# One core, two layers of graph attention: the last element's stores in four pieces, and new step lists for the first three and last two elements

## The chip, the cores and the metric

The kernel runs on one core of a Trainium2 chip. The metric is the device time of one execution in microseconds (us), lower is better. All data are fp32. The engines are called PE (TensorE, the matmuls), DVE (VectorE), ACT (ScalarE), POOL (GpSimd) and SP (SyncE, which here issues every transfer).

## The reference

`x` is 32 elements of 512 rows by 512 columns, `adj` 32 matrices of 512 by 512. Layer 0 is attention in 8 heads of 64 columns with a bias from the adjacency, an output projection, a residual and a layer norm. Layer 1 is graph attention on the same adjacency.

```python
# layer 0
q, k, v = x @ Wq.T + bq, x @ Wk.T + bk, x @ Wv.T + bv        # split into 8 heads of 64
logits = q @ k^T / 8 + log(clip(adj, 1e-8))                  # per head
out = (softmax(logits) @ v) @ Wo.T + bo
x = layer_norm(x + out) * gamma + beta
# layer 1
f = x @ fc_w.T + fc_b
logits = (f @ q_w + q_b) + (f @ k_w + k_b)^T
masked = logits + (1 - adj) * -1e9
atten = softmax(where(masked >= 0, masked, 0.01 * masked))
out = atten @ f + x
```

## The kernel before

The elements are worked through one after the other, with layer 1 one element and its output two elements behind layer 0. Products of 512 by 512 are done in seven half-size products instead of eight (Strassen's scheme), which is why there are many sums of quarters on DVE. The log of the adjacency is not formed: `exp(logits)` is multiplied by the clipped adjacency instead (`factor`, L947, on DVE).

Nothing is scheduled by a program: `fast` (L582) runs under a manual schedule, and each engine executes its instructions in the order in which they are written out. For each element two lists are run, by `first_two(b, order)` (L1427, heads 0 to 3) and `second_two(b, order)` (L1461, heads 4 to 7, and what belongs to the element before and the one after). A list is a string of step names; `perform` (L1405) calls one step after the other. A step issues between one and some 40 instructions on its engines. PE, DVE, ACT and SP each work strictly in order, so a step that waits holds everything that stands behind it on its engine. SP issues all transfers, so a load that must wait for its buffer holds the loads behind it.

Elements 2 to 30 use the lists `FIRST` and `SECOND`. Element 0 uses `FIRST0` and `SECOND0`, element 1 `FIRST1` and `SECOND1`, and element 31 `FIRST_LAST` and `SECOND_LAST`. The last one also does layer 1 of element 30 and, at its end, the whole of layer 1 of element 31.

The names that the change and the prediction use:

- `S0` to `S7`: the scores of a pair of heads for a quarter of the rows (PE, L935) and their exponential on ACT (L942, L944). `f` followed by head pair and quarter: `factor` (DVE, L950). `s` and `t`: the sums by which the softmax is divided (DVE, L962 to L973). `V0a`, `V0b`, `V0e` and so on: attention times values (PE, L1007) and its copy (ACT, L1016).
- `x`, `d`, `q`, `Q`, `p`, `v`: transposes, differences, and the products q and k of the pairs (`qm1` and on) and v (`vm1` to `vm7`) of the next element. `w` and `W`: the output projection. `n`, `k`, `u`: normalise rows (ACT, L414) and dot products for layer 1; `kst` and `kld`: the row of k goes to memory and comes back on all partitions (L448).
- `la`: the adjacency into `cT` in 16 transfers of 64 KB in pieces of 128 bytes; `c0` to `c3`: its turn (DVE, L683). `le0`, `le1`: the rows of the adjacency for layer 1 into `L` (L134), `mk0`, `mk1`: its masks (DVE, L455), `lg`, `lk`, `nm`, `ex`, `inv`, `nr`: layer 1's softmax. `ldn`: the rows of x for the residual. `lwv`, `lwk`, `lwq`, `lwo`, `lfc`: the weights; `lf`, `lv`, `lq0`, `lk0`, `lbo`, `lcc`, `lgamma`: vectors; `g`, `h`, `r`, `R`, `D`, `G`, `O`, `B`, `P`: sums of weights and folds of vectors into them.
- In the last list `om` and `oa`: the output product of element 29, `H`: the division of the last head pairs, `J`, `Z`, `Y`, `O`: layer 1 of element 30, names with a leading `x`: the layer-1 softmax of element 31, names with a leading `L` its products (`last_steps`, L1203), of which `Lo...` are the output steps of `last_out_steps` (L1319) and `Lot0` and on the stores. `rg0` to `rg2` compute a flag: if a sum fell outside a safe range, the elements are done again by `general`, which does not happen with these inputs.

Of the kernel before, what the change touches and what calls it, by code (L numbers as in the profile page):

```python
# [19 lines left out]
P = 128  # L20
# [10 lines left out]
def kernel(  # L31
# [550 lines left out]
    def fast(ctx):  # L582
# [736 lines left out]
        def last_out_steps(b, banks, x, fcs):  # L1319
# [25 lines left out]
            def store(row, count, j):  # L1345
                nc.sync.dma_start(
                    out=out[b][row * P : (row + count) * P, ts(j, H)].rearrange(
                        "(c p) d -> p c d", p=P),
                    in_=yb[:, row : row + count, ts(j, H)],
                )  # L1350
            return {
# [5 lines left out]
                "b11": lambda: add_rows(1, 1, "a"), "t0": lambda: store(2, 2, 1),  # L1357
                "b10": lambda: add_rows(1, 0, "a"), "t1": lambda: store(2, 2, 0),
                "m20": lambda: mul(2, "b", ns=(0,)),
                "b01": lambda: add_rows(0, 1, "c"), "t2": lambda: store(0, 2, 1),  # L1360
                "a000": lambda: add_rows(0, 0, "b", range(1)), "t3": lambda: store(0, 1, 0),
                "m21": lambda: mul(2, "d", ns=(1,)),
                "a001": lambda: add_rows(0, 0, "d", range(1, 2)), "t4": lambda: store(1, 1, 0),
# [145 lines left out]
        def end_steps(b, banks):  # L1509
# [48 lines left out]
            "ob11 ot0 ob10 ot1 om20 ob01 ot2 oa000 ot3 om21 oa001 ot4"  # L1558
# [37 lines left out]
            f30 f20 d3 lv1 r3 d2 f32 f23 f21 qcb qm6 f33 qm2 f31 qcq2 O0 mv0 qcq1
            vm5 V2a la V2b G1 qck2 vcb vc22 qm3 s20 qaq2 O1 qm7 dv0 vm6 V2e G2 vc12
            s21 vm3 va12 qak2 V3a Qm1 O2 Qcb c1 V3b s30 vm2 qm4 Qm6 qck1 Qm5 vm7 Qm2
            Qck2 c2 Qm4 s31 Qcq1 c3 Qm3 s32 s22 V3e va22 t20 Qcq2 vm4 G0 R0 sc01 Qm7
            Qck1 Qaq2 vc11 c0 sc00 Qak1 vc21 Qak2  # L1600
        """
        FIRST1 = """
            t21 S0 t30 t31 S1 S2 S3 S4 S5 mv2 S6 f00 S7 f01 f02 V0a qm1 f03 V0b G3
            R1 f13 f12 qcb qm6 V0e dv2 qm2 f10 qcq2 qcq1 f11 qm5 B1 qck2 P1 ldn P0
            P2 wseed s00 s01 qm3 qaq2 qm7 qak2 s02 V1a wm1 V1b t00 Qm1 fd wcb qm4
            Qcb sc20 sc21 qck1 fs wm2 ws11 R2 s10 Qm5 R3 s11 wm5 wa11 ws12 wm6 wm3
            wa01 wm7 t01 Qck2 wb01 wa00 ldx Qm6 Qm2 b0 wb11 s12 wm4 V1e b1 wa10 Qm4
# [25 lines left out]
            os12 V3e le0 H33 om7 oa11 H34 om3 Wal ob11 kld om4 ldn Wseed sc00 sc01
# [180 lines left out]
```

## Time and profile before

| what | us |
| --- | --- |
| median of three runs | 3275.07 (3274.25 to 3275.76) |
| profiled execution | 3278.6 |
| its span, first to last instruction | 3277.0 |
| PE busy | 3255.5 |
| DVE busy | 3077.4 |
| ACT busy | 1479.1 |
| mean granted PE clock | 0.999 of full speed |

The span is what the profile covers; the profiled execution's own time lies 1.6 us above it. A line of the timeline gives start and length in us, the engine, the line of the code, the operation, the tiles (output, then inputs) with their shape, how many instructions the group holds, and in brackets how long the engine was idle before it and who ended that. Matmuls overlap, so a group's starts tell more than its lengths: two groups of 16 matmuls of 256 columns follow each other at 1.73 us.

### The profile page before, as it was taken

How to read it: one execution, taken by the hardware profiler on the slowest of the kernel's cores; microseconds unless marked ns; L12 is line 12 of the kernel's file. 1: busy time of each engine (PE TensorE's matmuls, PEld its weight loads, DVE VectorE, ACT ScalarE, POOL GpSimd, SP SyncE). 2: the span in 40 equal slices, each digit the busy share in tenths (PEclk: the TensorE clock that was granted, in tenths of full speed). 3: DMA queues.
4: the chain of work that ended last, by engine and by line, in shares of the span. 5: the costliest groups of instructions: out<-in, count | busy, mean ns of one | idle time of the engine just before them, and what ended most of it. 6: DMA issues, size and time to landing. Idle time of an engine off the chain costs nothing.

```text
span 3277.0 us, 64102 instructions
## 1 busy us (share of the span) xinstructions
PE 3255.5 (99%) x25590; PEld 1886.2 (58%) x25590; DVE 3077.4 (94%) x5323; ACT 1479.1 (45%) x2770; POOL 1.4 (0%) x15
## 2 busy tenths in 40 slices
PE   9999999999999999999999999999999999999998
PEld 4555555555555555555556555555555555555555
DVE  7999999999999999999999999999999999999997
ACT  3445444445444354344444444544435444444443
POOL 0000000000000000000000000000000000000000
PEclk9999999999999999999999999999999999999999
DMA  5343433443433434334443345343343433443412
GB/s 133 51 70 86 74 83 66 77 96 64 89 68 69 96 70 89 73 68 86 89 71 84 67 76 96 64 91 73 62 96 72 88 76 64 86 92 69 86 46 78
DMA packets 917264, 256.46 MB, mean 78 GB/s; under 512 B 842720, under 2 KB 844768, under 8 KB 916960
## 3 DMA queue, kind: packets, MB, share of 16 engines
q1 hardware_dynamic: 916960, 252.30, 38.9%
q8 instruction: 204, 3.34, 0.4%
q14 instruction: 100, 0.82, 0.1%
HBM read 184.00 MB, written 36.72 MB: 67 GB/s over the span
## 4 chain that ended last, share of the span: by engine, by line
PE 97%; SPq 1%; DVE 1%; DMA 1%; ACT 0%; issue 0%; DVEq 0%
PE f L221 23%; PE mz L221 15%; PE my L221 15%; PE mx L221 15%; PE po L1007 14%; PE sc L935 7%; PE mx L935 2%; PE my L935 2%; PE mz L935 2%; SPq L620 0%; DMA L<-in_q_w_dram 0%; PE mx L350 0%; PE ps L1072 0%; SPq L134 0%; DMA L<-in_adj_dram 0%
## 5 line engine op out<-in xcount | busy, mean ns | idle before, releaser
L950 DVE SCALAR_TENSOR_TENSOR at<-cT,at 128x1024 f32<-128x1024 f32 x512 | 611.0, 1217 | 0.7 <-ACT at L944 0.5
L1007 PE MATMUL po<-at,v 128*64 128x512 f32 x2048 | 485.6, 595 | 0.7 <-ACT oT L1016 0.7
L739 ACT ACTIVATE qT<-f,bq 128x256 f32<-128x256 f32 x254 | 116.2, 472 | 816.7 <-PE f L221 816.6
L962 DVE TENSOR_TENSOR at<-at,at 128x1024 f32<-128x1024 f32 x378 | 455.2, 1211 | 3.7 <-PE po L1007 3.5
L1007 PEld LDWEIGHTS po<-at,v 128*64 128x64 f32 x2048 | 141.3, 137 | 225.0 <-issue 131.5
L221 PE MATMUL f<-xT,wq 128*64 128x256 f32 x2032 | 262.6, 379 | 0.5 <-ACT at L944 0.5
L944 ACT ACTIVATE at<-sc 128x1024 f32<-128x1024 f32 x256 | 259.7, 1079 | 4.6 <-PE sc L935 4.2
L221 PE MATMUL f<-T,qk_s 128*64 128x256 f32 x2032 | 256.3, 379 | 0.8 <-ACT kT L739 0.7
L935 PE MATMUL sc<-qT,kT 64*128 64x512 f32 x1024 | 242.3, 589 | 0.0
L221 PEld LDWEIGHTS f<-xT,wq 128*64 128x64 f32 x2032 | 145.7, 137 | 102.7 <-issue 36.7
L221 PEld LDWEIGHTS f<-T,qk_s 128*64 128x64 f32 x2032 | 145.5, 137 | 87.9 <-issue 17.1
L739 ACT ACTIVATE kT<-f,bk 128x256 f32<-128x256 f32 x254 | 120.5, 474 | 119.5 <-PE f L221 118.1
L935 PEld LDWEIGHTS sc<-qT,kT 64*128 64x128 f32 x1024 | 99.8, 187 | 120.3 <-issue 76.5
L966 DVE STREAM_TRANSPOSE at<-at 128x1024 f32<-128x1024 f32 x126 | 154.8, 1229 | 1.1
L973 DVE TENSOR_REDUCE ks<-at 128x32 f32<-128x1024 f32 x126 | 152.2, 1208 | 1.0
L935 PE MATMUL so<-qT,kT 64*128 64x512 f32 x256 | 137.1, 615 | 0.0
L935 PE MATMUL mx<-qT,kT 64*128 64x512 f32 x256 | 132.7, 598 | 1.2 <-ACT v L802 0.7
L935 PE MATMUL mz<-qT,kT 64*128 64x512 f32 x256 | 132.6, 598 | 0.0
L935 PE MATMUL my<-qT,kT 64*128 64x512 f32 x256 | 132.4, 597 | 0.2 <-ACT v L802 0.2
L221 PE MATMUL f<-T,wk 128*64 128x256 f32 x1016 | 131.3, 379 | 0.0
L221 PE MATMUL f<-xT,wk 128*64 128x256 f32 x1016 | 131.3, 379 | 0.0
L221 PE MATMUL f<-xT,qk_s 128*64 128x256 f32 x1016 | 131.3, 379 | 0.0
(391 smaller groups left out, 6397.7 us busy)
## 6 DMA issues: line engine op xcount, KB each, us to landing
cT<-in_adj_dram SPq DMA_DIRECT2D x512, 64.0 KB
R<-d SPq DMA_DIRECT2D x126, 256.0 KB
x<-in_x_dram SPq DMA_DIRECT2D x124, 256.0 KB
L<-in_adj_dram SPq DMA_DIRECT2D x62, 512.0 KB
n<-in_x_dram SPq DMA_DIRECT2D x31, 1024.0 KB
out_dram<-yb SPq DMA_DIRECT2D x62, 512.0 KB
eP<-L SPq DMA_DIRECT2D x480, 64.0 KB
w<-dk SPq DMA_DIRECT2D x32, 256.0 KB
```

The source lines that it names most:

```text
L221: nc.tensor.matmul(to[ts(h, DK)], left[:, ts(h, DK)], right, start=start, stop=stop, skip_group_check=True,)
L739: nc.scalar.activation(of(w, half), ps[bank], AF.Identity, bias=bias)
L935: nc.tensor.matmul(parts[j], s["kT", p][rows, ts(kc, P)], s["qT", p][rows, :], start=True, stop=True,)
L944: nc.scalar.activation(at, sc, AF.Exp, scale=SCALE)
L950: nc.vector.scalar_tensor_tensor(at, cT[:, kc, :].unsqueeze(1).to_broadcast([P, 2, N]), ADJ_MIN, at, ALU.max, ALU.mult,)
L962: nc.vector.tensor_add(to, to, s["at", p, kc])
L966: nc.vector.transpose(flat, flat)
L973: nc.vector.tensor_reduce(ks.rearrange("p h m -> p (h m)"), flat.rearrange("p (a k) -> p a k", k=BL), AX.X, ALU.add,)
L1007: nc.tensor.matmul(s["po", p][j * DK : (j + 1) * DK, :], s["v"][h // 4][:, kc, ts(h % 4, DK)], s["at", p, kc][:, j, :], start=(kc == 0), s ...
```

## The change

The stores of the last element go out in four pieces instead of five, three of them changed in shape: rows 2 and 3 whole, row 1 right, row 0 whole, row 1 left (a "row" is 128 rows of the matrix). The six special lists are laid anew. The steps are the same but for the store that is gone; some steps stand in another list (the loads `lv1`, `lf0`, `lv2`, `lgamma` and the folds `r2`, `D6`, `D7`, `O2`, `R0`, `G0`, `G2`).

```diff
-            def store(row, count, j):
+            def store(row, count, cols):
                 nc.sync.dma_start(
-                    out=out[b][row * P : (row + count) * P, ts(j, H)].rearrange(
+                    out=out[b][row * P : (row + count) * P, cols].rearrange(
                         "(c p) d -> p c d", p=P),
-                    in_=yb[:, row : row + count, ts(j, H)],
+                    in_=yb[:, row : row + count, cols],
                 )
+            whole, left, right = slice(0, D), slice(0, H), slice(H, D)
...
-                "b11": lambda: add_rows(1, 1, "a"), "t0": lambda: store(2, 2, 1),
-                "b10": lambda: add_rows(1, 0, "a"), "t1": lambda: store(2, 2, 0),
+                "b11": lambda: add_rows(1, 1, "a"), "b10": lambda: add_rows(1, 0, "a"),
+                "t0": lambda: store(2, 2, whole),
                 "m20": lambda: mul(2, "b", ns=(0,)),
-                "b01": lambda: add_rows(0, 1, "c"), "t2": lambda: store(0, 2, 1),
-                "a000": lambda: add_rows(0, 0, "b", range(1)), "t3": lambda: store(0, 1, 0),
+                "b01": lambda: add_rows(0, 1, "c"), "t2": lambda: store(1, 1, right),
+                "a000": lambda: add_rows(0, 0, "b", range(1)), "t3": lambda: store(0, 1, whole),
                 "m21": lambda: mul(2, "d", ns=(1,)),
-                "a001": lambda: add_rows(0, 0, "d", range(1, 2)), "t4": lambda: store(1, 1, 0),
+                "a001": lambda: add_rows(0, 0, "d", range(1, 2)), "t4": lambda: store(1, 1, left),
...
         FIRST0 = """
-            X0 X1 X2 X3 E1 E0 E2 E3 A0 lwv A1 d0 g0 lwk vm1 vm5 vcb d1 g3 d3 lgamma
-            la3 lwq lf2 g1 vm6 vc22 vm2 d2 vc12 lq0 g2 g4 la2 vm7 vm3 la0 va22 c3
-            vm4 vc21 lbo vc11 lwo S0 c2 va12 S1 S2 S3 h0 pm1 h4 pm5 h1 c0 h3 pcb f00
-            lfc pck2 r0 pm6 h2 lf1 D0 pm2 pm4 lv0 pm3 la1 pcq2 pcq1 D1 pm7 pck1 D2
-            paq2 pak1 S4 r1 c1 S5 pak2 S6 S7 D3 f01 Bq f03 f02 V0a V0b V0e f10 qm1
-            qcb qm5 D4 qck2 f13 f12 f11 qm6 qm2 s00 qm3 D5 s01 qcq1 B0 s02 D6 lv2
-            qcq2 qm7 qak2 r2 D7 lk0 V1a V1b V1e qaq2 t00 s10 lcc qm4 qck1 Qm1 Qcb
-            s11 s12 Qm5 Qm6 Qm2 Qck2 Qm4 Qcq1 t01 Qcq2 Qm3 Qm7 Qck1 ldx Qak1 Qak2
-            Qaq2
+            X0 X1 X2 X3 E0 E1 E3 E2 A0 lwv g0 A1 g1 d0 la1 d1 vm1 g3 lwk d2 vcb g2
+            vm5 g4 lwo h0 vm6 d3 vm2 vc12 lwq vm7 vc11 vc22 vm3 va22 la0 vm4 vc21 S0
+            c0 va12 S1 S2 h4 S3 pm1 h1 pm5 la2 h2 pcb pck2 lfc pm6 lf1 h3 lf0 pm2 D0
+            pcq1 pm4 pcq2 D1 la3 c3 lf2 pm3 f03 pck1 c1 paq2 lv0 pm7 pak1 S4 pak2 S5
+            S6 S7 Bq qm1 f01 c2 r0 qm5 lbo D2 f10 qcb qm6 f11 qm2 f12 f00 V0a f02
+            f13 V0b D3 s00 qcq1 lv1 qcq2 qm7 B0 lcc s01 qck2 V0e qak2 s02 qm3 qaq2
+            t00 V1a V1b lq0 Qm1 s10 D4 qm4 Qcb ldx s11 Qm6 D5 qck1 V1e Qm5 Qck2 Qm2
+            Qcq2 Qm4 s12 Qm3 Qcq1 t01 lk0 Qck1 Qm7 r1 Qak2 Qaq2 Qak1
         """
         SECOND0 = """
-            S0 x0 t10 x3 lf0 S1 x1 t11 S2 d0 f22 S3 S4 S5 S6 S7 Oq x2 d1 qm1 vm1 qm5
-            f30 f20 d3 lv1 r3 d2 f32 f23 f21 qcb qm6 f33 qm2 f31 qcq2 O0 mv0 qcq1
-            vm5 V2a la V2b G1 qck2 vcb vc22 qm3 s20 qaq2 O1 qm7 dv0 vm6 V2e G2 vc12
-            s21 vm3 va12 qak2 V3a Qm1 O2 Qcb c1 V3b s30 vm2 qm4 Qm6 qck1 Qm5 vm7 Qm2
-            Qck2 c2 Qm4 s31 Qcq1 c3 Qm3 s32 s22 V3e va22 t20 Qcq2 vm4 G0 R0 sc01 Qm7
-            Qck1 Qaq2 vc11 c0 sc00 Qak1 vc21 Qak2
+            x0 S0 S1 t10 t11 f20 S2 x1 S3 S4 f21 d0 S5 lv2 S6 S7 f22 x3 Oq f31 D6 x2
+            d1 qm1 qm5 f30 mv0 dv0 f23 qck2 qcb r3 O0 V2a vm1 qm3 qm6 V2b d3 f33 qm2
+            G1 vcb vm6 qcq1 qcq2 qaq2 V2e D7 qm7 V3a Qm1 s20 Qcb f32 qak2 sc01 d2
+            V3b vc12 qm4 qck1 vm7 s30 Qm6 vm5 vc22 la Qm5 Qck2 c0 Qm2 Qcq2 Qm4 Qcq1
+            sc00 c1 s21 Qm3 s22 c2 Qm7 V3e O1 Qck1 c3 va22 s31 t20 Qak1 vm4 vm3 vc21
+            vm2 s32 va12 vc11 Qaq2 Qak2
         """
         FIRST1 = """
-            t21 S0 t30 t31 S1 S2 S3 S4 S5 mv2 S6 f00 S7 f01 f02 V0a qm1 f03 V0b G3
-            R1 f13 f12 qcb qm6 V0e dv2 qm2 f10 qcq2 qcq1 f11 qm5 B1 qck2 P1 ldn P0
-            P2 wseed s00 s01 qm3 qaq2 qm7 qak2 s02 V1a wm1 V1b t00 Qm1 fd wcb qm4
-            Qcb sc20 sc21 qck1 fs wm2 ws11 R2 s10 Qm5 R3 s11 wm5 wa11 ws12 wm6 wm3
-            wa01 wm7 t01 Qck2 wb01 wa00 ldx Qm6 Qm2 b0 wb11 s12 wm4 V1e b1 wa10 Qm4
-            Qcq1 b2 Qm3 b3 Qcq2 Qck1 Qaq2 Qm7 Qak2 Qak1
+            fd t30 S0 S1 t21 t31 mv2 f01 S2 S3 S4 f00 S5 f02 G0 S6 O2 S7 f03 B1 ldn
+            P0 f10 wseed V0a V0b qm1 dv2 s00 f12 s01 qcb V0e f13 qm5 qck2 qm6 qm2
+            qm3 P1 qcq2 f11 P2 qcq1 s02 wm1 qm7 V1a wcb qak2 r2 G2 V1b qaq2 G3 qm4
+            sc21 sc20 fs ws11 R0 R3 Qm1 R1 t00 wm5 wm2 ldx wa11 wm6 ws12 qck1 Qcb
+            t01 wa00 wm3 R2 Qm6 wa01 s10 wb01 wm7 Qm5 s11 Qck2 wb11 b0 Qm2 Qcq1 b1
+            s12 wm4 Qcq2 wa10 b2 b3 Qm4 Qm3 Qck1 Qaq2 Qm7 Qak1 Qak2 V1e
         """
         SECOND1 = """
-            x0 n0 t10 S0 x2 t11 mv0 S1 S2 x1 S3 n2 f23 d0 S4 f20 n1 x3 S5 le1 k0 S6
-            n3 f32 vm1 k1 k2 n4 k3 vm5 u0 S7 qm1 k4 le0 qcb d1 vcb qm5 d3 qck2 kst
-            u1 f33 kld qm6 u3 u2 qm3 vm6 f21 f22 qm2 u4 V2a vm2 dv0 mk1 qcq2 f31 V2b
-            vc22 V2e f30 vc12 s20 mk0 qcq1 d2 lg0 lg1 lg2 lg3 lk0 V3a vm3 nm ex0 lk3
-            qm7 ex3 vc11 V3b vm7 va12 lk1 ex1 qaq2 la qak2 lk2 Qm1 qm4 Qcb ex2 s30
-            sc00 qck1 inv Qm5 nr0 nr3 va22 nr1 s31 sc01 Qm6 Qm2 nr2 Qck2 Qm4 vm4 s21
-            Qcq2 c0 s22 c2 Qcq1 c1 Qm3 Qck1 bl t20 Qaq2 s32 Qm7 Qak2 Qak1 vc21 c3
-            V3e
+            t10 n0 x0 x1 S0 S1 t11 S2 n2 S3 S4 S5 S6 f22 n3 d0 n1 n4 f21 le1 vm1 S7
+            qm1 x3 qcb vcb k1 qm5 x2 k0 d1 qm6 k2 d2 k3 qck2 u0 qm2 k4 vm6 u2 d3 mv0
+            le0 kst f32 qcq2 kld mk0 qcq1 qm3 u1 qm7 vm5 vc22 vc12 f30 qak2 qaq2 u3
+            dv0 Qm1 f20 f33 Qcb u4 f23 lg0 lg1 f31 mk1 qm4 V2a V2b V2e vm2 qck1 Qm6
+            Qm2 V3a Qm5 lk1 lg2 lg3 lk2 lk3 nm s20 ex3 ex1 ex2 la c0 lk0 ex0 sc00
+            Qcq2 Qck2 s21 V3b inv vm7 nr1 Qm4 Qcq1 Qm3 s22 va22 s30 V3e c1 s31 vm3
+            Qm7 nr0 nr2 vm4 va12 Qck1 Qaq2 s32 nr3 vc21 bl t20 Qak1 c2 lgamma Qak2
+            sc01 c3 vc11
         """
         FIRST_LAST = """
-            t21 S0 t30 f00 S1 S2 f01 t31 S3 S4 S5 S6 S7 V0a qm1 f02 y0 e2 qcb e0 qm5
-            e1 qck2 e3 qm6 qm2 zt1 qm3 qcq2 zm1 zs1 f10 qaq2 zcb f13 zm5 zA21 Qm1
-            zE11 mv2 zA11 zE12 zc22 zm2 zm6 dv2 qcq1 zE21 f03 qm7 zc12 V0b f11 zm7
-            fd Qcb y1 s00 zA12 f12 Qm6 za22 V0e s01 sc21 sc20 fs qak2 zc11 V1a zm3
-            za12 zm4 zc21 V1b wseed wm1 s10 s11 V1e ws11 ldn s02 wcb t00 wm5 wm2
-            wa11 qm4 ws12 wm6 wa01 wm3 wa00 qck1 wb01 t01 b0 wm7 wb11 Qm2 s12 b1 Qm5
-            Qcq1 Qck2 wm4 wa10 b2 Qm4 Qcq2 Qm3 b3 Qm7 Qck1 Qaq2 Qak2 Qak1
+            S0 S1 t21 f00 t30 f01 S2 S3 S4 S5 t31 f02 S6 S7 V0a qm1 y0 e1 qm5 qcb
+            qm6 qm2 qcq1 e0 mv2 zm1 f03 e2 V0b e3 zs1 zt1 zcb qcq2 zm5 zE11 zA21 dv2
+            zE12 qck2 qm3 qaq2 f11 zA11 zm2 f10 f13 y1 zA12 zE21 Qm1 qm7 Qcb Qm6 V0e
+            zm6 V1a sc21 zc12 zc22 s00 qak2 zm7 za22 zm3 sc20 zc11 f12 zm4 fd V1b
+            za12 ldn s01 zc21 fs Qm2 wseed s10 s11 wm1 ws11 wm5 wcb s02 wm6 wm2 t00
+            qm4 Qcq1 wa11 wa01 qck1 ws12 s12 wm7 wm3 wa00 t01 Qm5 Qck2 wb11 wm4 wb01
+            b0 Qm4 b1 wa10 Qcq2 b2 Qm3 V1e Qck1 b3 Qaq2 Qm7 Qak1 Qak2
         """
         SECOND_LAST = """
-            n0 S0 S1 S2 S3 t10 zd S4 S5 oseed f21 f20 n1 S6 n2 f23 f31 t11 f22 S7 n3
-            V2a zs f30 om1 H20 k1 V2b n4 k0 mv0 ocb k3 om2 k2 f32 k4 V2e u0 os11 u1
-            H30 H21 kst om6 V3a u3 u2 dv0 u4 f33 H31 H22 H32 H23 V3b oa01 om5 H24
-            os12 V3e le0 H33 om7 oa11 H34 om3 Wal ob11 kld om4 ldn Wseed sc00 sc01
-            Wfd mk0 Wm1 Wfs lg1 le1 lg0 Wcb lk1 Ws11 lk0 mk1 lg3 lg2 Wm5 Wm6 Wm2
-            Wa01 nm Wa11 lk2 ex1 ex0 Wm7 Ws12 Lal lk3 Wb11 ex2 ex3 inv nr2 oa10 Wm3
-            Wa00 oa00 nr0 ob01 Wb01 Wm4 Wa10 nr1 nr3 J0 J1 J2 b0 J3 b1 b2 b3 xle0
-            xmk0 xn0 xn2 xn4 xn1 xn3 xk1 xk3 xk0 Z0 Z1 Z2 xk2 xle1 ost1 ost0 yn
-            Oseed xk4 xkst xu1 y1 Z3 xmk1 xkld Om1 xu0 xu3 xu2 xu4 Yd y0 Ys xlg0
-            Os11 xlg1 Om5 Ocb xlg2 Om6 Oa11 xlg3 Oa01 xlk3 xnm Om2 xex3 xlk0 Om7
-            Os12 xlk2 xlk1 xex0 Ob11 xex2 xex1 xinv Om3 LN2 xnr0 Om4 xnr3 Lp0 Oa10
-            xnr1 LN0 Lp1 LN1 xnr2 Oa00 Lp2 Lp3 Le0 Ob01 Le1 Le2 Lm1 Le3 LT0 Lm5 Lcb
-            LT1 LT3 Lm6 Lc12 LT2 Lc22 Lm7 Ly Lm2 Lc11 LN3 La22 Lm4 Lm3 La12 LZ2 LZ0
-            Ost1 Lc21 Loseed Lom1 Lom4 Locb LZ1 Lom6 LZ3 Loa01 rg0 Lom5 Lom21 Loa001
-            rg1 Loa10 Lom7 Loa11 Lob11 Lob10 rg2 Ost0 Lom3 Lob01 Lom20 Lot4 Lot0
-            Loa000 Lot1 Lot2 Lot3
+            n0 zd S0 f20 S1 S2 t10 S3 f22 n1 f21 zs f23 S4 S5 S6 ldn t11 k0 n2 k1 n3
+            k2 oseed S7 V2a H20 mv0 f30 n4 V2b k3 om1 u0 os11 ocb u1 u2 u3 dv0 H21
+            u4 V2e f31 k4 om6 om2 oa01 om5 os12 H22 kst f32 le0 H30 oa11 om7 f33 H23
+            V3a H31 H32 ob11 sc00 Wal sc01 kld V3b om3 V3e om4 xle0 Wfd H24 xle1 le1
+            H33 Wseed mk0 Lal H34 Wfs lg0 lg1 lk0 lk1 Wm1 Wm5 Ws11 Wcb Wm6 mk1 Wm2
+            lg3 lg2 Wa01 Wm7 nm ex1 lk2 ex0 Wa11 Ws12 lk3 Wb11 Wm3 oa10 ex2 ex3 inv
+            nr0 ob01 nr2 nr1 Wm4 Wa00 Wb01 oa00 ost0 Wa10 nr3 J0 b0 b1 b2 J1 J2 b3
+            xn0 J3 xmk1 xn2 xk1 xn1 xk0 xn4 xk3 ost1 xn3 yn Z0 xk2 xk4 xkst xu1 xu0
+            xkld Z1 Z2 y0 Yd Oseed xu3 xu2 y1 Z3 Om1 xu4 xmk0 Ys xlg1 Os11 Om5 Ocb
+            xlk1 Om6 xlg0 xlg3 Oa11 Oa01 xlg2 xlk3 xnm xex3 xex1 Om2 Os12 xlk2 Om7
+            xlk0 Om3 Ob11 LN0 xex2 Om4 xex0 xinv xnr0 Oa10 xnr1 Ob01 LN2 Lp0 xnr2
+            Ost1 Lp1 xnr3 Lp2 Lp3 Le0 Oa00 Le1 Le2 Le3 LT0 Lm1 Lm5 Ost0 LT1 LN1 rg0
+            Lcb Lm6 LT2 LN3 LT3 Lc12 Lc22 Ly Lm7 Lm2 La22 Lm4 Lm3 La12 LZ0 Lc11 LZ1
+            Lc21 Loseed Lom1 Lom4 rg1 LZ2 Locb LZ3 Loa10 Lom6 Loa01 Lom5 Lom7 Loa11
+            Lob11 Lob10 rg2 Lot0 Lom3 Lob01 Lot2 Lom20 Lom21 Loa000 Lot3 Loa001 Lot4
         """
```

## The prediction

> **What bounds the kernel now.** I read the page first (busy shares, chain), then the windows of the stretches whose lists change, then the waits of the tensor engine (PE), and last the timelines around each wait and around the last loads and stores.
>
> ```profile
> PE 3255.5 (99%) x25590; PEld 1886.2 (58%) x25590; DVE 3077.4 (94%) x5323; ACT 1479.1 (45%) x2770; POOL 1.4 (0%) x15
> PE 97%; SPq 1%; DVE 1%; DMA 1%; ACT 0%; issue 0%; DVEq 0%
> 0.00:45.00 45.00, 39.21 (x236) 21.76 (x240) 23.28 (x38) 15.16 (x26) 1.36 (x15) 1.00 0.83 215
> 110.00:220.00 110.00, 106.16 (x772) 58.44 (x770) 103.49 (x179) 52.97 (x98) 0.00 (x0) 0.98 0.35 58
> 220.00:320.70 100.70, 100.61 (x800) 58.41 (x798) 95.51 (x166) 45.81 (x86) 0.00 (x0) 1.00 0.40 79
> 3200.00:3230.00 30.00, 27.42 (x148) 14.97 (x148) 26.13 (x64) 16.93 (x32) 0.00 (x0) 1.00 0.25 91
> ```
>
> The last four lines are windows: stretch, length, then busy time of PE, weight loads, DVE, ACT, POOL, the granted clock, DMA share and GB/s. A steady element (220 to 320.7) keeps PE busy 100.61 of 100.70 us. The change touches no steady list, so those 29 elements (2 to 30) give nothing and take nothing. What can move lies at the two ends: PE is idle 5.8 us in the first 45 us, 3.84 us in 110:220 (mostly element 1's second list), 2.58 us in 3200:3230, and the stretch after the last matmul. The waits say for what:
>
> ```profile
> PE my L221 <- ACT at L942: 2.2, 1, 2.2
> PE pw_a L221 <- DVE n L866: 1.5, 1, 1.5
> PE pw_a L221 <- DVE oT L862: 0.9, 1, 0.9
> PE my L221 <- DVE eT L1258: 0.8, 1, 0.8
> ```
>
> Read: what PE ran when the wait ended, who released it, total us, times, longest. All are single events, so each belongs to one place in one special list. PE does the same work per list before and after (sums of its rows are equal list by list: 56.85, 39.81, 40.26, 37.91, 50.00 and 98.92 us), so the time moves only by waits, the clock and the drain.
>
> **Part 1, element 1's second list: about -2.5 us.** The dearest wait is followed by slow matmuls:
>
> ```profile
> 152.61 1.02 PE L935 MATMUL sc<-qT,kT 64*128 64x512 f32 x4
> 155.81 3.62 PE L221 MATMUL my<-wv,xT 128*64 128x256 f32 x16 [2.17 <-ACT at L942]
> 159.26 1.89 PE L221 MATMUL mz<-v_s,T 128*64 128x256 f32 x16
> 152.25 0.85 ACT L414 ACTIVATE n<-n,rt,rstd 128x512 f32<-128x512 f32 x1
> 153.91 0.87 ACT L414 ACTIVATE n<-n,rt,rstd 128x512 f32<-128x512 f32 x1
> 155.10 0.66 ACT L942 ACTIVATE at<-my 128x512 f32<-128x512 f32 x1
> ```
>
> vm1 (the first value product, 155.81) writes the bank "my" that the exponential of S5 still reads (155.10 to 155.76); ACT reaches that one late because two normalise rows (n2 and n1, 0.85 and 0.87 us) stand ahead of it in its queue. After the wait the 16 matmuls take 3.62 us where the next such group takes 1.89: half clock, 1.73 us more, which is also the 0.98 of the window. By starts against the pitch of a group that does not wait (1.73 us for 16 of these matmuls), the losses of the list are 2.6 at 155.81, 0.45 at 163.33, 1.06 at 174.58 and 184.96 each, 0.3 and 0.8 before 192.50, and 0.5 at 200.05; with the 1.73 that is 8.5 us.
>
> In the changed list one normalise row fewer stands ahead of that exponential, so vm1 loses about 1 us less, 1.6. But the new order does not run free: walking it with the rows' durations (DVE: factor 1.22, sum 1.21, transpose 1.21, reduce 1.19; ACT: 0.47 to 1.08) I find DVE behind at V2a and V2b (waits for f20 and f23, about 0.75 and 0.6), qm5 about 0.5, and vm4 standing last, so that the next element's S0 waits for its sum, about 0.9. V0b in element 1's first list, with O2's 1.95 us moved ahead of it, waits about 0.4. That is 1.6 + 0.75 + 0.6 + 0.5 + 0.9 + 0.4 = 4.75 in place of 8.5. DVE limits the rest of it: it ends the last turn of the adjacency (c3) at 192.8 instead of 194.9 by the walk, so element 2's first value product comes at 197.5 instead of 200.05. I take that -2.5; bounds -1 (DVE further behind than walked) and -3.75 (the difference of the losses in full).
>
> The half clock is uncertain. In these rows an idle time of 2.17 us is followed by 3.4 us at half clock, and one of 1.49 us at 3206 is followed by a group of 1.95, at full clock. With about 1.5 us left I expect none. [...]
>
> **Part 2, the loads of element 0: 0.** wv, wk, wq, wo, fc and the four pieces of the adjacency go through SP in another order, with the same bytes. PE's waits there (0.69 at 30.25, 0.49 at 34.45, 0.53 at 41.30) are for ACT and DVE, none for a load, and I find the same three in the new order. Cover: before, the loads landed wv 13.1, wk 16.4, la3 18.1, wq 21.8, la2 26.3, la0 28.2, wo 34.6, fc 37.4, la1 39.7. Keeping these lengths, the new order puts wq at 23 to 25, la0 25 to 27, la2 27 to 29.5, fc 30 to 33, la3 33 to 37. la3's turn (c3) now stands ahead of the DVE sums that S4 needs (41.30); it must land by about 38.8. If it lands later, each us costs one. The steps that change lists (the loads lv1, lv2, lf0 and lgamma, small rows; the folds O2, r2, R0 on DVE and G0, G2 on ACT, now in element 1's first list; D6 and D7 in element 0's second) keep their rows and stand in stretches where DVE is ahead of PE, apart from the O2 counted above; uncovered, each fold would cost at most its own 1 to 2 us.
>
> **Part 3, the last two elements: about -3.5 us.** The tail waits for rows of the adjacency:
>
> ```profile
> 3191.40 1.90 PE L221 MATMUL mz<-fc,third 128*64 128x256 f32 x16
> 3191.61 0.41 SPq L134 DMA_DIRECT2D L<-in_adj_dram  x1
> 3192.57 0.43 SPq L134 DMA_DIRECT2D n<-in_x_dram  x1
> 3196.79 0.38 SPq L134 DMA_DIRECT2D L<-in_adj_dram  x1
> 3203.42 0.69 DVE L455 TENSOR_SCALAR L<-L 128x1024 f32<-128x1024 f32 x1 [1.56 <-DMA L<-in_adj_dram]
> 3206.23 1.95 PE L221 MATMUL pw_a<-wo,w 128*64 128x256 f32 x16 [1.49 <-DVE n L866]
> ```
>
> le1 (3196.79) waits for om4 to free its half of L, then shares the DMA engines with the 1-MB ldn (issued 3192.57) and the two xle pieces behind it; the mask mk1 runs at 3203.42, 6.6 us after the issue. DVE works in order: behind mk1 stand the logits and the sum (L866) that PE needs at 3206.23. The change issues ldn right after S6, about 3171, le0 after om5, which now stands earlier on PE (about 3185), the k row 6.5 us earlier, both xle pieces at about 3187, and le1 last and alone, still at 3196.7 because om4 still ends there. ldn reads into a tile whose last reader is in the list before, so nothing holds SP there. Alone, 512 KB take about 3.5 us (the k row, 256 KB, took 4.27 beside other loads): mk1 at about 3200.3, 3.1 us earlier. The two waits (0.86 at 3201.06 and 1.49 at 3206.23, 2.9 us by the pitch) go. What is late next: turn_e (J, about 1.0, unchanged), the first fc product behind the evictions Le (0.46 + 0.77 at 3242.9 and 3244.3, by the pitch 1.8; about half of it stays, as Le1 now follows Le0), and 0.69 at 3249.95, unchanged. -2.9 - 0.9 is -3.8; I take 3.5, bounds -2 (the DVE work behind mk1 refills half) and -4.5.
>
> **Part 4, the stores: -0.3.**
>
> ```profile
> 3268.72 1.03 PE L221 MATMUL mx<-fc,L 128*64 128x256 f32 x8
> 3269.80 0.42 DVE L1343 TENSOR_TENSOR qk_s<-mx,qk_s 128x256 f32<-128x256 f32 x1 [0.17 <-PE mx L221]
> 3265.34 5.25 SPq L1346 DMA_DIRECT2D out_dram<-qk_s  x5
> ```
>
> The last matmul ends at 3269.75, the last sum at 3270.22, SP's fifth store at 3270.59, the span at 3277.0: 7.25 us of drain. The same 1 MB goes as 640 pieces instead of 1024 (512 KB and 256 KB in 2-KB rows, twice 128 KB in 1-KB rows). The last matmul, its 0.42-us sum and a last store of 128 KB remain; the two halves of rows 2 and 3 leave together, 0.67 us later than the first half did. What is saved is one SP issue (about 0.4) at most on the way; bounds +0.5 (a larger piece ahead of the last) and -1.5 (fewer pieces).
>
> **Sum.** -2.5 + 0 - 3.5 - 0.3 = -6.3 against the profiled execution (3278.6 us, span 3277.0): span 3270.7. The profiled execution is 3.5 us above the median of the timed runs (3275.07); I do not know whether the half clock falls in all of those. I count its 1.73 us at half: -6.3 + 0.9 = -5.4, and 3275.07 - 5.4 = 3269.7.
>
> **Rivals.** (a) *Slower: a load ends late in element 0's new order.* DVE runs in order, so c3 waiting for la3 holds everything behind it. Against the -5.4 above it has to cost 12 us to be slower by over 0.2% (6.55 us, about what a measurement of this kernel can tell from no change), that is la3 landing at about 51 instead of 33 to 37: 39.7 was the last landing before. 3282, 14 in 100, the lesser forms of it (la3 at 40 to 45) falling into "same". (b) *Element 1 gains nothing:* DVE, 103.49 of 110 us busy, just moves its wait from vm1 to V2a, V2b and S0. Only the tail counts: -3.5 - 0.3, 3271.3. 25 in 100. (c) *More:* element 1's losses in full (-3.75), -4.5 at the tail, -0.8 at the stores: -9, about 3266. 18 in 100. (d) *The tail gains nothing:* the k row and the mask come early, but DVE's 26.13 busy us of 30 refill it; element 1 alone, -2.5 + 0.9 - 0.3, about 3273. 10 in 100. The forecast, 3269.7: 33 in 100.
>
> **Range and chances.** Its ends: 3264.5 (case c with -1.5 of the stores) and 3278 (case d with a late load of 5 us). Faster by over 0.2% means below 3268.5: c, nearly half of the forecast, and little of b: 0.37. Slower (above 3281.6): 0.14. The rest, 0.49, is within.
>
> **What would show it.** Right: in 150:157 the wait of vm1 shrinks to about 1.5 and the group takes 1.9; mk1 about 3.1 us earlier against the last list's start and no wait of pw_a for DVE; in 0:45 the same 5.8 us of PE idle. Wrong: a DMA among the releasers in the first 50 us; new waits of PE for DVE at L950 or L962 between 150 and 200 above 2.5 us in all; half clock anywhere; a drain over 8 us after the last matmul.

## The result, and the profile after

After takes 3269.97 us (median of 22 runs, 3268.39 to 3271.02), before in the same comparison 3275.82 (22 runs, 3273.40 to 3278.42): 5.85 us less, ratio 0.9982 with a 95% interval of 0.9976 to 0.9988. The prediction said 3269.7, 5.4 below its median of before. The profiled execution of after takes 3270.89 us with a span of 3268.8.

First the busy line, then the same windows as before (stretch, length, then busy time of PE, weight loads, DVE, ACT and POOL, granted clock, DMA share, GB/s). Element 1's stretch has 107.25 us of PE in place of 106.16 and the full clock, and the tail 29.62 of 30 in place of 27.42. PE is idle for 6.06 us of the first 45 in place of 5.79; the difference lies in the wait for the first rows of x (4.3 us in all in place of 4.0).

```profile
PE 3252.9 (100%) x25590; PEld 1886.5 (58%) x25590; DVE 3077.4 (94%) x5323; ACT 1476.1 (45%) x2770; POOL 1.4 (0%) x15
...
0.00:45.00 45.00, 38.94 (x232) 21.61 (x232) 22.20 (x35) 14.90 (x26) 1.35 (x15) 1.00 0.96 221
110.00:220.00 110.00, 107.25 (x792) 60.50 (x790) 107.61 (x191) 55.71 (x104) 0.00 (x0) 1.00 0.37 61
3200.00:3230.00 30.00, 29.62 (x174) 16.33 (x172) 27.20 (x69) 17.47 (x33) 0.00 (x0) 1.00 0.13 45
```

PE's waits in after (what PE ran, who released it, total, times, longest). The two waits of the output projection for DVE (1.5 and 0.9) are gone, so are two of 0.7 for ACT in element 1 (`po L1007` and `f L221`). The one for the exponential is 1.2 in place of 2.2. One has grown, `my L935`, 0.7 (before 0.2), and one is new, 0.6 for a factor.

```profile
PE my L221 <- ACT at L942: 1.2, 1, 1.2
PE my L935 <- ACT v L802: 0.7, 1, 0.7
PE my L221 <- ACT L L1276: 0.7, 1, 0.7
PE po L1007 <- DVE at L950: 0.6, 1, 0.6
PE my L221 <- DVE eT L1258: 0.2, 1, 0.2
```

The timelines at the places that the prediction showed: vm1, the first wait for a factor, the loads of the tail with mask and projection, and the end. The group of vm1 takes 1.95 us (before 3.62, half clock); the loads now go out over 33 us instead of 6; the mask at 3197.53 follows its load's issue by 3.68 us (before 6.63), and the projection at 3200.54 no longer waits.

```profile
153.05 1.27 PE L935 MATMUL sc<-qT,kT 64*128 64x512 f32 x4
155.57 1.95 PE L221 MATMUL my<-wv,xT 128*64 128x256 f32 x16 [1.25 <-ACT at L942]
169.98 3.65 PE L1007 MATMUL po<-at,v 128*64 128x512 f32 x16 [0.56 <-DVE at L950]
189.84 0.69 PE L935 MATMUL my<-qT,kT 64*128 64x512 f32 x1 [0.69 <-ACT v L802]
```

```profile
3160.81 0.39 SPq L134 DMA_DIRECT2D n<-in_x_dram  x1
3182.83 0.40 SPq L134 DMA_DIRECT2D L<-in_adj_dram  x1
3185.13 0.34 SPq L448 DMA_DIRECT2D w<-dk  x1
3185.52 0.93 SPq L134 DMA_DIRECT2D cT<-in_adj_dram  x2
3193.85 0.37 SPq L134 DMA_DIRECT2D L<-in_adj_dram  x1
3197.53 0.69 DVE L455 TENSOR_SCALAR L<-L 128x1024 f32<-128x1024 f32 x1 [0.36 <-DMA L<-in_adj_dram]
3200.54 1.90 PE L221 MATMUL pw_a<-wo,w 128*64 128x256 f32 x16
```

```profile
3262.39 1.03 PE L221 MATMUL pw_o_d<-fc,L 128*64 128x256 f32 x8
3263.47 0.42 DVE L1343 TENSOR_TENSOR qk_s<-pw_o_d,qk_s 128x256 f32<-128x256 f32 x1 [0.44 <-PE pw_o_d L221]
3261.10 3.16 SPq L1346 DMA_DIRECT2D out_dram<-qk_s  x4
```

Where the 8.16 us of span went, by positions of the same matmul in both traces: element 2's value product starts at 196.91 in place of 200.05 (-3.14); the steady elements differ by +0.19; from a group of element 29 to the last matmul's end it is 345.41 in place of 348.78 us (-3.37); from there to the end of the span 5.40 in place of 7.24 (-1.84). The profiled execution of before is a dear one: it lies 2.8 us above the median of the timed runs, that of after 0.9.

Two things blur such positions from execution to execution. At the start the clock becomes full anywhere from 7.9 to 12.7 us into the profiled executions, and a later one puts element 2 later, by about half a us for each us between after and ldn_late, which have the same first lists (after: full from 12.68 us, element 2 at 196.91; ldn_late: 9.38 and 195.19). The table gives the positions of element 2 for a full clock from 12.5 us on. And a stretch of 3.41 us at half clock after vm1's wait comes in some executions only; it costs about 1.7 us (vm1's group takes 3.62 us in before, 1.95 in after) and has a column of its own. The time behind the last matmul is split where the last store has landed, that is at the last of the 16 reports that it leaves in the trace (before: 3274.06).

| kernel | us, median | element 2's value product, start | half clock after vm1 | element 29 to last matmul | last matmul to the last store's landing | landing to end |
| --- | --- | --- | --- | --- | --- | --- |
| before | 3275.82 | 200.07 | yes | 348.78 | 4.31 | 2.93 |
| after | 3269.97 | 196.82 | no | 345.41 | 3.82 | 1.58 |
| head_only | 3272.92 | 196.79 | no | 348.48 | 4.30 | 1.51 |
| ends_only | 3273.47 | 198.47 | no | 345.59 | 3.77 | 3.45 |
| old_stores | 3269.85 | 196.78 | no | 345.49 | 3.65 | 1.51 |
| ldn_early | 3273.69 | 198.21 | no | 345.83 | 4.04 | 3.28 |
| row_behind | 3274.97 | 197.86 | no | 348.55 | 4.42 | 2.93 |
| row_ahead | 3270.14 | 198.63 | yes | 345.43 | 3.69 | 1.59 |
| x_first | 3278.44 | 205.75 | 10.2 us, earlier | 345.69 | 3.61 | 1.58 |
| vm4_early | 3270.20 | 196.43 | no | 345.62 | 3.92 | 1.58 |
| more_pe | 3274.71 | 201.14 | yes | 348.55 | 4.27 | 1.51 |
| ldn_late | 3270.33 | 196.75 | no | 345.93 | 3.82 | 1.58 |
| vm2_vm4 | 3270.91 | 196.88 | no | 345.55 | 3.83 | 1.58 |

more_pe's 201.14 can't be compared: its full clock came at 9.54 us, but 1.1 us of what that gave was lost in a longer wait for DVE at 40.90 (1.63 in place of 0.53); as it stands in the trace, element 2 starts at 199.66.

The medians of the experiments are of 11 runs; before took 3275.64, 3276.37 and 3276.16 us in the three groups in which they ran. The interval of a ratio is about 0.0009 to each side (some 3 us), so terms below that are read from the traces' positions. After ran in another group than the experiments; a difference between medians that is taken from it also holds the groups' own difference, up to 0.7 us by the medians of before.

### The profile page after: what moved, and what is told of

It reads as the page before. It is cut to its first block, busy times and chain, and to the rows that moved or that the text cites. A ratio compares the mean times of both kernels' runs of the same rounds, so it can differ in the third digit from the quotient of the medians.

```text
span 3268.8 us, 64099 instructions
## 1 busy us (share of the span) xinstructions
PE 3252.9 (100%) x25590; PEld 1886.5 (58%) x25590; DVE 3077.4 (94%) x5323; ACT 1476.1 (45%) x2770; POOL 1.4 (0%) x15
## 4 chain that ended last, share of the span: by engine, by line
PE 97%; DVE 1%; ACT 0%; DMA 0%; issue 0%; SPq 0%; DVEq 0%; ACTq 0%
PE f L221 23%; PE mz L221 15%; PE my L221 15%; PE mx L221 15%; PE po L1007 13%; PE sc L935 6%; PE mx L935 2%; PE mz L935 2%; PE my L935 2%; PE mx L350 0%; DVE at L950 0%; PE mz L350 0%; PE ps L1072 0%; ACT at L942 0%; DVE at L962 0%; DMA n<-in_x_dram 0%
## 5 line engine op out<-in xcount | busy, mean ns | idle before, releaser
L1007 PE MATMUL po<-at,v 128*64 128x512 f32 x2048 | 485.2, 595 | 0.6 <-DVE at L950 0.6
L1007 PEld LDWEIGHTS po<-at,v 128*64 128x64 f32 x2048 | 141.3, 137 | 225.2 <-issue 131.1
L221 PE MATMUL f<-xT,wq 128*64 128x256 f32 x2032 | 262.6, 379 | 0.5 <-ACT at L944 0.5
L221 PE MATMUL f<-T,qk_s 128*64 128x256 f32 x2032 | 256.8, 379 | 0.2
L935 PE MATMUL sc<-qT,kT 64*128 64x512 f32 x1024 | 241.8, 589 | 0.0
L221 PEld LDWEIGHTS f<-xT,wq 128*64 128x64 f32 x2032 | 145.6, 137 | 103.8 <-issue 36.3
L221 PEld LDWEIGHTS f<-T,qk_s 128*64 128x64 f32 x2032 | 145.4, 137 | 87.6 <-issue 17.1
L935 PEld LDWEIGHTS sc<-qT,kT 64*128 64x128 f32 x1024 | 100.1, 187 | 119.5 <-issue 75.3
L935 PE MATMUL so<-qT,kT 64*128 64x512 f32 x256 | 137.1, 615 | 0.0
L935 PE MATMUL mx<-qT,kT 64*128 64x512 f32 x256 | 132.7, 598 | 1.2 <-ACT v L802 0.7
L935 PE MATMUL my<-qT,kT 64*128 64x512 f32 x256 | 132.4, 597 | 0.7 <-ACT v L802 0.7
L935 PE MATMUL mz<-qT,kT 64*128 64x512 f32 x256 | 132.6, 598 | 0.0
L221 PE MATMUL f<-xT,qk_s 128*64 128x256 f32 x1016 | 131.3, 379 | 0.0
L221 PE MATMUL f<-T,wk 128*64 128x256 f32 x1016 | 131.2, 379 | 0.0
L221 PE MATMUL f<-xT,wk 128*64 128x256 f32 x1016 | 131.2, 379 | 0.0
```

Of the source, the lines that this page charges most:

```text
L221: nc.tensor.matmul(to[ts(h, DK)], left[:, ts(h, DK)], right, start=start, stop=stop, skip_group_check=True,)
L935: nc.tensor.matmul(parts[j], s["kT", p][rows, ts(kc, P)], s["qT", p][rows, :], start=True, stop=True,)
L1007: nc.tensor.matmul(s["po", p][j * DK : (j + 1) * DK, :], s["v"][h // 4][:, kc, ts(h % 4, DK)], s["at", p, kc][:, j, :], start=(kc == 0), s ...
```

## The experiments

**head_only and ends_only: the change in two halves.** The lists of after for elements 0 and 1, and the lists of element 31 with the new stores, each put alone into before.

```diff
 head_only:  FIRST0, SECOND0, FIRST1, SECOND1 as after; the rest as before
 ends_only:  FIRST_LAST, SECOND_LAST, last_out_steps as after; the rest as before
```

> Before, with the four new lists of elements 0 and 1; the lists of element 31 and the stores as before. Theory of the prediction: -2.5 us, of which the half clock is part, so -1.6 to -2.5 in the timed median. Rival (DVE takes back what element 1's waits give): 0 within 0.5. Rival (the two profiles' starts of element 2's values, 200.05 and 196.91, tell it all): -3.1. In its profile, the start of element 2's value product: 196.9 by the last, 197.5 by the first, 200 by the second.

> Before, with the two new lists of element 31 and the new stores; the lists of elements 0 and 1 as before. Theory of the prediction: -3.5 - 0.3 = -3.8 us. Rival (the drain is worth as much as the two profiles show, 7.25 against 5.40 us after the last matmul): -3.4 - 1.85 = -5.25. Together with the run of the four first lists alone it should add up to the whole, -5.85, if the parts are independent.

Measured: -2.72 us (ratio 0.9993, 0.9984 to 1.0002) and -2.17 us (0.9994, 0.9985 to 1.0003), the second less than either number expected. By the medians alone neither half is clear of no change; the positions are sharper. The first lists move element 2 to 196.8; ends_only and ldn_early, which have the old first lists and happened to meet no half clock, stand at 198.47 and 198.21. So the first lists save 1.4 to 1.7 us of waits, and 1.7 more where the half clock would have fallen. The last lists save 3.2 (345.59 against 348.78). The halves add up to 4.9, 1 us short of the whole, which is less than the interval of either. One reason shows in the last column: from the landing to the end head_only takes 1.51 us and ends_only 3.45, so that part comes with the first lists, not with the stores; more_pe takes it up.

**old_stores: the five pieces in after.**

```diff
 old_stores (in after; the last argument of store is the half of the columns, 0 left and 1 right)
-                "b11": lambda: add_rows(1, 1, "a"), "b10": lambda: add_rows(1, 0, "a"),
-                "t0": lambda: store(2, 2, whole),
+                "b11": lambda: add_rows(1, 1, "a"), "t0": lambda: store(2, 2, 1),
+                "b10": lambda: add_rows(1, 0, "a"), "t1": lambda: store(2, 2, 0),
 ...            t2: store(1, 1, right) -> store(0, 2, 1), t3: store(0, 1, whole) -> store(0, 1, 0),
 ...            t4: store(1, 1, left) -> store(1, 1, 0); the sums in the order of after
```

> After, with the five stores of before in their old shapes and places behind the same sums; the order of the sums as after. Theory of the prediction: +0.3 us (bounds -0.5 to +1.5) against after, so -5.5 against before. Rival (the shape of the stores makes the shorter drain): +1.85 against after, -4.0 against before, and 7 us or more from the last matmul to the end of the span instead of 5.4.

Measured: 3269.85 us, 0.1 below after, and 3.65 + 1.51 us of drain against 3.82 + 1.58. The four wider pieces are worth nothing; the rival falls. In all kernels with the last list of after the last store has landed 3.6 to 3.9 us after the last matmul, in all with the old one 4.0 to 4.4, whatever the stores' shapes: 0.5 us in before against after. The last store is issued 0.50 us after the last matmul in both and lands 3.81 us after its issue in before, 3.32 in after. The two lists differ there in the order of the last sums: in before 896 KB of the 1 MB are issued from 3267.69 on, 2.1 us before the last matmul ends, in after the 512 KB of rows 2 and 3 go at 3261.10, 2.3 us before it, and 512 KB are left. That the smaller crowd is why the last store lands sooner is likely, but not tested by itself.

**ldn_early and ldn_late: one load.**

```diff
 ldn_early (in before):  ... n1 S6 +ldn n2 f23 ...   le0 H33 om7 oa11 H34 om3 Wal ob11 kld om4 -ldn Wseed
 ldn_late  (in after):   ... S5 S6 -ldn t11 k0 ...   sc00 Wal sc01 kld +ldn V3b om3 ...
```

> Before, with the one step ldn (the 1-MB load of the rows of x) moved from behind the k row to behind S6 in the last list; nothing else. Theory of the prediction (le1 shares the DMA engines with ldn, mask and sums stand behind it): le1 lands 2 to 3 us sooner, the waits of 0.86 and 1.49 us at the sums of the output projection go in part, -1.5 to -2.9 us. Rival (le1 shares with the two xle pieces behind it as much, and the k row is late anyway): less than 0.7.

> After, with the one step ldn moved back from behind S6 to behind the k row in the last list. Theory (ldn alone makes the tail's gain, -2.95 us of PE time when it was moved in before): +2 to +3 us against after, with the waits for DVE at the sums of the output projection back. Rival (the new order of the other loads and products covers it): less than +0.7.

```profile
3200.32 1.90 PE L221 MATMUL pw_a<-wo,w 128*64 128x256 f32 x16
```

Moving it in before takes both waits of the projection away (ldn_early's line above has no wait, in before it was 1.49 us): element 29 to the last matmul is 345.83, 2.95 us less, nearly the tail's whole gain, and the median is 1.95 lower (0.9994, 0.9985 to 1.0003). Moving it back in after costs only 0.5 us on that measure and 0.36 in the median, where +2 to +3 was expected. My theory that this load alone makes the gain was wrong in that direction. The profile of ldn_late shows why: counted from the same group of element 29, le0, the k row and the 1-MB load behind them go out 5.9, 4.1 and 4.1 us earlier than in before, while le1 goes at the same point. So le1 is issued 8.28 us after the 1-MB load instead of 4.22, and of the two waits 0.17 us is left.

```profile
3183.45 0.34 SPq L448 DMA_DIRECT2D w<-dk  x1
3183.85 0.42 SPq L134 DMA_DIRECT2D n<-in_x_dram  x1
3192.13 0.37 SPq L134 DMA_DIRECT2D L<-in_adj_dram  x1
3199.17 1.95 PE L221 MATMUL pw_a<-wo,w 128*64 128x256 f32 x16 [0.17 <-DVE n L866]
```

Either move is enough, the load's or the new order of the other steps of the last list (which of those steps matter was not split further). What the two have in common is that the 1-MB load has landed by about the time le1 goes out. It landed 5.1 us after le1's issue in before and 0.2 us after it in ldn_late, and long before it in after and ldn_early; le1 took 6.60, 4.21, 3.66 and 3.67 us from issue to landing. The two xle pieces count for little: in ldn_early they are issued right behind le1, as in before.

**row_behind and row_ahead: the wait of vm1 and the half clock.**

```diff
 row_behind (in before): ... f20 -n1 x3 S5 le1 k0 S6 +n1 n3 f32 vm1 ...
 row_ahead  (in after):  ... n2 S3 S4 +n3 S5 S6 f22 -n3 d0 n1 n4 f21 le1 vm1 ...
```

> Before, with one step of element 1's second list, the normalise row n1 on ACT, moved from ahead of S5 to behind S6. Theory of the prediction: vm1 waits about 0.8 to 1 us less and there is no half clock; in the profile the start of element 2's value product moves from 200.05 by 1 to 2.7 us; in the timed median -0.8 to -1.7. Rival (DVE holds PE at the next waits, 174.58 and 184.96, whatever vm1 does): within 0.4 of before.

> After, with one normalise row (n3) moved ahead of S5 in element 1's second list, so that two rows stand ahead of the exponential that vm1 waits for, as before the change. Theory of the prediction: vm1 waits 2.1 instead of 1.25 us; +0.4 to +0.9 us against after without a half clock, up to +2.6 with one. [...] Rival (DVE sets the pace behind it): within 0.4 of after.

With one row fewer, vm1's wait in before falls by 0.7 us, from 2.17 to 1.47, and element 2 comes at 197.86, against 198.2 to 198.5 for the same lists without half clock: 0.35 to 0.6 us of it arrive. With one row more in after the wait grows by the same 0.7, from 1.25 to 1.94, and the profile has the half clock again (the first line below: the group of 16 matmuls takes 2.78 us); without its 1.7 us element 2 stands at 196.9, where it stands in after. The second line is from ends_only: there the wait of before, 2.17 us, is followed by a group at full clock.

```profile
153.71 2.78 PE L221 MATMUL my<-wv,xT 128*64 128x256 f32 x16 [1.94 <-ACT at L942]
155.45 1.95 PE L221 MATMUL my<-wv,xT 128*64 128x256 f32 x16 [2.17 <-ACT at L942]
```

The medians moved by -1.4 and +0.2 us, the second less than the +0.4 at least that was expected. So in after the wait of vm1 is taken back behind it, as the rival said, and in before about half of it or more is not. Behind vm1 the half clock came with waits of 2.17 us (before, more_pe) and 1.94 (row_ahead), and in no profile with one of 1.47 or less; in ends_only and ldn_early it did not come with 2.17 either.

**x_first: the price of a late load.** The load of element 1's x goes ahead of la3, whose four transfers then land at 42.8 to 43.8 us instead of 35.0 to 36.4.

```diff
 x_first (in after): ... D1 +ldx la3 c3 ...   ... ldx removed behind Qcb
```

> After, with the load of element 1's x (1 MB, landing 41.7 to 49.1 us in after) moved ahead of la3 in element 0's first list, so that la3 (landing 36.4) lands about 46. Theory of the prediction (c3 holds DVE in order, S4 slips 1 us for each us beyond about 38.8): S4 at about 48 to 49 instead of 41.5, +6 to +8 us against after, -0 to +2 against before. Rival (the delay is caught up, as DVE has 7 per cent of slack in the following stretch): +2 or less against after.

```profile
44.03 0.71 DVE L683 STREAM_TRANSPOSE cT<-cT 128x512 f32<-128x512 f32 x1 [8.68 <-DMA cT<-in_adj_dram]
47.38 1.22 PE L935 MATMUL mx<-qT,kT 64*128 64x512 f32 x1 [6.71 <-DVE kT L743]
42.73:52.97 10.24, 5.58 (x14) 2.51 (x16) 8.34 (x13) 2.22 (x5) 0.00 (x0) 0.50 0.63 82
```

The two timeline lines and the window show it: c3 starts at 44.03 instead of 36.57 (7.46 us later), S4 at 47.38 instead of 41.53 (5.85 later). In after DVE stood idle for 1.47 us behind c3 (until 40.70), so the limit for c3's start was about 38.0; the 5.99 us beyond it became 5.85 at S4. Behind the wait of 6.71 us PE runs at half clock for 10.24 us, and element 2 comes 8.9 us late in all; the median is 3278.44 us, 8.5 above after and 2.1 above before of its group (3276.37), a little more than was expected, which had no half clock in it. The rival of slack falls.

**vm4_early and vm2_vm4: what the waits left in element 1 are worth.**

```diff
 vm4_early:  ... vm3 +vm4 Qm7 nr0 nr2 -vm4 va12 ...
 vm2_vm4:    the same, and  ... qm4 +vm2 V2a V2b V2e -vm2 qck1 ...
```

> After, with vm4 set ahead of Qm7 in element 1's second list, so that the copy of the value product which element 2's first scores wait for (0.69 us at 189.84 in after, 1.07 against the pitch) lies beside the 8 matmuls of Qm7. Theory of the prediction (PE's waits in this list are the time): -0.8 to -1.0 us against after. Rival (DVE ends the turn of the adjacency, c3, at the same time and element 2's first factors come no sooner): within 0.3 of after.

> After, with vm4 ahead of Qm7 as before and also vm2 ahead of V2a in element 1's second list, so that the 16 matmuls of vm2 lie beside the wait for the factor f20 (0.56 us at 169.98 in after). Theory (PE's waits are the time): element 2's value product 0.8 to 1.3 us earlier than in after at the same time of the first full clock, -0.8 to -1.3 in the median. Rival (DVE sets the pace; vm4 alone gave -0.4 in the profile and nothing in the median): within 0.5 of after.

Element 2 starts at 196.43 and 196.88 (after 196.82), the medians are 3270.20 and 3270.91. Both targeted waits went (0.69 at 189.84, 0.56 at 169.98), and others came in their place (lines of vm2_vm4):

```profile
181.53 1.08 PE L221 MATMUL f<-T,wk 128*64 128x256 f32 x8 [0.65 <-ACT kT L739]
190.96 1.13 PE L935 MATMUL sc<-qT,kT 64*128 64x512 f32 x4 [0.39 <-DVE kT L743]
```

Neither version beats after: PE's waits here are not the time itself. In after DVE is busy 107.61 of the 110 us, so the likely reading is that they are where PE falls into step with DVE and ACT; no run with a faster DVE tests it.

**more_pe: the late end of the old first lists.** In all four profiles with the old first lists and no step added (before, ends_only, ldn_early, row_behind) PE stands still late in its last few instructions and goes on 1.42 to 1.53 us after the end of the last 16-KB packet of the queue that the page lists as `q8 instruction` (before: packet until 3275.48, the other engines are through at 3275.54, PE goes on at 3276.94). In the eight profiles with the new first lists it does not. PE's stream has 51670 to 51673 recorded instructions with the old ones, 51674 to 51677 with the new, and in the four the stop comes after instruction 51668 or 51669. So, the idea to be tested, a longer stream might put the stop ahead of PE's last own wait (L1767). That wait is not for the last store, as the expectation below has it: in all 13 profiles PE passes it 0.25 to 0.99 us before the last store has landed (before: 3273.81 and 3274.06), behind its branch on the flag, which ends 1.42 to 1.55 us after another 16-KB packet (before: 3273.75 and 3272.20). It is SP that waits for the stores: in before it goes on at 3274.08, 0.02 us after the last landing.

```diff
 more_pe (in before):
             def turn(c):
                 for i in range(DC):
+                    if c == 0:
+                        nc.tensor.transpose(pt[i][:2, ts(c, P)], ident[:, :2], ident)
                     nc.tensor.transpose(pt[i][:, ts(c, P)], s["n"][:, c, ts(i, P)], ident)
```

> Before, with four more tiny transposes on PE (2 columns by 128, into banks that are overwritten at once) at the very start, while PE waits for the first rows of x; nothing else. They add 8 instructions to PE's stream. Theory (a late fetch of PE's last 16-KB piece of instructions: in the four runs with the old first lists PE stands still 1.4 to 1.9 us shortly before its last instructions and resumes 1.4 to 1.5 us after the last 16-KB packet; the new first lists shift that point ahead of the wait for the last store): the stop falls before that wait, from there to the end of the span 1.9 to 2.3 us instead of 3.2, and -0.9 to -1.4 us in the median against before, less up to 0.3 for the transposes. Rival (the first lists shorten the end in some other way): the end as before, 0 to +0.3 us.

Four useless transposes at the start (51677 instructions in the profile) take the late stop away: from PE's last own wait to the end it is 2.00 us in place of 3.18, from the last landing to the end 1.51 in place of 2.93. The median is 3274.71 against 3276.16 us, -1.45; it fits those 1.42, but its ratio (0.9993, 0.9984 to 1.0002) is not clear of no change. The shift is shown in the profile. What PE waits for at the stop is not: that it is the packet is my reading of the order of events, the same at the stop in four profiles and at the branch in 13.

## Why the prediction was right, and where its sizes were off

**Element 1 (-2.5, bounds -1 and -3.75).** Measured -3.14 in the profiles (-3.25 in the table): 1.4 to 1.7 of waits, by the two profiles without half clock, and the rest half clock. The walk named the new waits nearly, by starts against the pitch: vm1 loses 1.81 (forecast 1.6), V2a 0.89 (0.75), the scores behind vm4 1.07 (0.9), the q product 0.43 (0.5); those for V2b and V0b did not come. c3 ends at 193.05 (192.8), element 2 starts at 196.91 (197.5). The size came near because DVE's pace was in it: the losses alone gave -3.75, and vm2_vm4 shows that PE's waits alone mislead.

**The half clock, counted at half.** Four profiles have the old wait of vm1, about 2.2 us: before and more_pe show the half clock, ends_only and ldn_early do not. So half was a fair count for the profiles. For the timed runs there is a bound: in 22 of the 93 timed executions of before in the three groups the granted clock is 1.000, which leaves hardly any room for 3.41 us at half clock: they alone would make it 0.99948 (1.71 us lost of a span of about 3274), which three digits give as 0.999. In the profile of before PE was busy for 36 per cent of the 3.41 us ahead of the half clock, in that of row_ahead for 43 (last section).

**Element 0's loads (0).** Right: the three waits are 0.69, 0.49 and 0.53 us as before. The loads landed as forecast: wq 24.1 (23 to 25), la0 26.6 (25 to 27), la2 28.3 (27 to 29.5), fc 32.5 (30 to 33), la3 36.4 (33 to 37). The rival of the late load was real with a price near one us per us as stated (5.85 for 5.99 in x_first), plus the half clock, which the prediction had not priced; the limit for c3's start was about 38.0.

**The tail (-3.5).** Measured -3.37. On before's time, which is 2.95 us later here: ldn out at 3163.8 (forecast about 3171), le0 at 3185.8 (3185), the k row 4.1 us earlier (6.5), le1 at 3196.8 (3196.7) and the mask 2.9 us earlier (3.1); no wait of the projection for DVE; the first fc product loses 1.2 in place of 1.8 (0.9), the last wait 0.69 is unchanged. The cause was told too narrowly: ldn_late shows that the rest of the new order is enough without ldn's early place. The 4.27 us that the prediction has for the k row is not what the trace shows: issued at 3192.18, it landed 5.70 us later. Its 3.5 us for 512 KB alone was near (le1 took 3.66 in after).

**The stores (-0.3, bounds +0.5 and -1.5).** The term that was mis-sized: the drain fell by 1.84 us in the profiles, beyond the bound. The shape of the pieces is worth nothing (old_stores). 0.5 comes with the new last list, in which half of the output goes out earlier, and 1.35 from a place that the prediction did not look at: PE's late stop, which went with the longer instruction stream of the new first lists. The step that failed is "The last matmul, its 0.42-us sum and a last store of 128 KB remain", so the drain stays: it took the 7.25 us for one fixed block and did not split it at the landing of the last store.

Sized by the profiles the parts give 1.6 + 3.4 + 1.8 = 6.8 us without the half clock and 8.5 with it; the medians show 5.85, with an interval of 3.9 to 7.9. About 0.4 us of the difference lies outside the span: the timed executions are longer than their spans by 2.04 us in after and by 1.62 to 1.66 in before (medians), and no run says why. That the total was so near the forecast is partly luck: the too small term of the drain stands against a median that moved less than the sum of the parts. Whether the timed runs have the 1.8 us of the drain in full stays open.

**The range.** Its lower end, 3264.5, counts the stores twice: case c has -0.8 for them already, and with -1.5 in its place it would be 3265.4. Nothing hangs on it here.

## What to carry to other kernels

Where one engine is busy nearly all the time, look at the two ends, and ask at each wait what would be next late: removing a PE wait in a stretch in which DVE is busy 98 per cent moved the wait (vm2_vm4: 0.56 and 0.69 us went, 0.65 and 0.39 came), while moving one 1-MB load out of the way of a smaller late one took 2.95 us away (ldn_early). Split a drain into the last computation, the landing of the last store, and what the engines still do after it; here the last two moved each by itself, by 0.5 and 1.35 us.

## What the runs showed of the hardware that was not expected

- **Half clock came after stretches of 3.41 us in which PE was busy for 29 to 43 per cent.** In before the granted clock is full from 12.46 us on for 143.36 us, then half for 3.41, full for 3112.95, and half in the drain; 143.36 and 3112.95 are 42 and 912 times 3.413, and the full stretch of after, 3252.90, is 953 times that. In the 3.41 us ahead of a fall PE was busy for 36 per cent in before at 155.82 and for 29 at 3272.19, for 37 in after at 3265.58, for 40 in x_first at 42.73; the waits of row_ahead (1.94 us) and more_pe (2.17) make it 43 and 36. Cut into stretches of that length from the first full clock on, before and after have no other one at full clock under 56 per cent, and the clock stayed full behind those (56 for the 1.49-us wait at 3206 of before, 64 for the wait of 1.25 in after). In ends_only the same wait of 2.17 us as in before is split over two such stretches, one busy for 51 per cent, and the group behind it ran at full clock (1.95 us).
- **Half clock at the start.** The matmuls start at half clock, as their lengths show: in before the first 8 of 512 columns, at 7.99, take 5.90 us, the next 8, at 13.73, 3.60, with the full clock from 12.46 on. PE was busy for 57, 88 and 100 per cent of the three stretches of 3.41 us ahead of that, in after for 57, 87 and 100 (full from 12.68). In x_first the half clock ran on, from 42.73 to 52.97, behind a stretch in which PE was busy for 64 per cent (46.14 to 49.56).
- **Four useless matmuls took 1.4 us off the end of the profile.** From the last landing to the end it is 2.93 us in before and 1.51 in more_pe. In the four profiles in which PE stands still behind its last own wait, after recorded instruction 51668 or 51669, it is 2.93 to 3.45 us, in the nine others 1.51 to 1.59.
- **The same store bytes in 640 or 1024 pieces** took about the same drain: 5.40 us in after and 5.16 in old_stores.
